# An edge-attention layer on one core: gathers two to three pairs ahead in two buffers, attributes loaded from ScalarE's queue

## The chip, the cores and the metric

The kernel runs on one core of one Trainium2 chip. The metric is the time of one execution in device microseconds (us); a kernel's time is the median of its runs. The engines are named as in the profile: PE (TensorE, matmuls), PEld (its weight loads), DVE (VectorE), ACT (ScalarE), POOL (GpSimd) and SP (SyncE, which here only issues DMAs). "SPq" and "ACTq" are the DMA queues of SP and ACT.

## The reference

A graph layer over 12500 nodes of 128 channels and 400000 edges, which come sorted by their target (dst), while their sources (src) are in no order:

```python
h = jnp.maximum(_layernorm(x), 0)
msg_src = h @ w_src + b_src
msg_dst = h @ w_dst
message = msg_src[edge_src] + msg_dst[edge_dst]
rad_w = mlp3(edge_attr_32)            # 32 -> 64 -> 64 -> 128, silu between
message = message * edge_weight1 * rad_w
message = message @ w_sep + b_sep     # 128 -> 256
alpha, value = split(message.reshape(E, 8, 32))    # 16 + 16 in each of 8 heads
score = einsum('ehk,ahk->eh', smooth_leaky_relu(alpha), alpha_dot)
att = segment_softmax(score, edge_dst)
out = segment_sum(value * att, edge_dst).reshape(N, 128)
return x + out @ w_proj + b_proj
```

(Names shortened; mlp3 and split stand for what the reference writes out.) For each edge a row of msg_src has to be fetched by an index (the gather), a row of msg_dst is found nearby, because the targets are sorted, and 32 attributes go through a small network.

## The kernel before

Three phases follow each other. Up to about 110 us the two node tables are made (t_src, t_dst) and the limits of the windows of targets are found. Then `windows()` goes over the edges; this phase ends near 5700 us and is the one that the change touches. Last, the sums of windows that share targets are put together and the output product is made.

`windows()` works on 400 pairs k of 1000 edges. A pair has two sections f of 500 edges, each with a window of at most 64 rows of targets, and a section is four tiles of 125 edges. The order of the work is written out by hand in `step(k)`, which runs for k = -5 to 399 and then for a few steps more: every call in it appends its instructions to the engines' queues, in that order. A step handles several pairs at different stages:

- Loads for later pairs, issued by SP at the step's start: the edge weights `load_w(k + 3)` (L718), the two windows of target rows `load_md(k + 3)` (tile md, L720 to L724; SP reads each window's start from a table first), for every second k the target indices `load_d` (tile d_b), and the attributes `load_e(k + 6)` (tile e_t, L705 to L707; 1000 runs of 128 bytes).
- `gather(k, f)` (L739 to L747): four indirect DMAs issued by POOL (L744), each of which fetches 125 rows of t_src into the tile gs0 or gs1. It is called for pair k + 4, section 1, after the transposes of pair k, section 1, and for pair k + 5, section 0, after those of pair k + 1, section 0.
- The network of the attributes: `e_T` for k + 3 (PE transposes of e_t into m1, ACT copy), `mlp1` for k + 2 (L763, ACT silu into h, L766), `mlp2` for k + 1 (L778, L781) and `mlp3` for k (L795), whose result DVE multiplies by the edge weights (rad, L799).
- `split_md` (L726 to L737): the target rows of k + 1 are split in three bf16 parts, two by ACT (L730, L735) and two subtractions by DVE (L733, L737).
- `sources` (L808): PE transposes the gathered rows into the PSUM tiles pm0, pm1; `message` adds the target rows by one-hot products (L816), and DVE makes mT from pm and rad (L821).
- `alphas(k, f)`: the product pa (L825), ACT's silu into sl (L827), DVE's al (L829); it is called for section 0 in the middle of the step and for section 1 near its end. `scores` (every second step) makes the scores of two pairs and SP writes them out (L841).
- The softmax runs per group of 8 pairs (MP = 8). 12 steps later (pair c = k - 12) `values` (V, L908; pvx, L910), `one_hot` and `sums` (L919; ACT copy ob, L923) are made, and SP stores the sums, `store_win` (L927) and `store` (L931, tile agg).

Each tile's name has a fixed number of buffers (`bufs`): a new tile of that name reuses the oldest buffer, and its first writer waits until the former tile's last reader is done. Before the change e_t has 4, md has 4, gs0 and gs1 have 4 each. A DMA also waits for the one that was issued eight earlier of its kind (SP's and ACT's together, POOL's apart), since eight completion semaphores are used in turn.

The order in `step` around the change is:

```python
if has(k + 3):
    load_w(k + 3)
    load_md(k + 3)
if k % 2 and has(k + 3):
    load_d((k + 3) // 2)
if has(k + 6) and k >= -4:
    load_e(k + 6)
```

Of the kernel before, what the change touches and what calls it, by code (L numbers as in the profile page):

```python
# [21 lines left out]
F32 = mybir.dt.float32  # L22
# [8 lines left out]
P = 128  # L31
C = 128
# [14 lines left out]
TS = 4  # L47
# [9 lines left out]
def gnn_kernel(ctx: ExitStack, tc: tile.TileContext, a: dict, out: bass.AP):  # L57
    nc = tc.nc
# [69 lines left out]
    def zero(i):  # L128

        av = agg[0:N, :].rearrange("(p t) c -> p (t c)", p=RP)  # L130
        nc.sync.dma_start(out=av[:, i * zc * ROW:(i + 1) * zc * ROW], in_=z)
        if i == 0:
            nc.sync.dma_start(out=agg[N:N + W, :], in_=z[:W, 0:ROW])
# [527 lines left out]
    def windows():  # L661
        src_t = src.rearrange("(t p) -> t p", p=T)
        dst_t = dst.rearrange("(t p) -> t p", p=T)
        ea_t = ea.rearrange("(k j p) c -> k p j c", j=8, p=T)
        dst_p = dst.rearrange("(k f e) -> f k e", f=2, e=SEC)
        ew_p = ew.rearrange("(k e) o -> o k e", e=PR)
        with tc.tile_pool(name="wk2", bufs=2) as sp, tc.tile_pool(name="ps", bufs=1, space=PSUM) as pp, \
                tc.manual_schedule(), ExitStack() as held:
            lp = held.enter_context(tc.tile_pool(name="ld", bufs=2))
            prep, e_g, d_g, w_g, md, gath = {}, {}, {}, {}, {}, {}  # L670
# [4 lines left out]
            def prep_load(u):  # L675
                t0 = u * P
                ri = lp.tile([P, 2, T], I32, name="ri")
                rb = lp.tile([P, 1], I32, name="rb")
                nc.sync.dma_start(out=ri[:, 0, :], in_=src_t[t0:t0 + P, :])
                nc.sync.dma_start(out=ri[:, 1, :], in_=dst_t[t0:t0 + P, :])  # L680
                at = dst_t[t0:t0 + P, 0:1]
                (step, _), *_ = at.ap
                at = bass.AP(at.tensor, at.offset, [[step * TS, P // TS], [0, TS], [1, 1]])
                with nc.allow_non_contiguous_dma(reason="a word per tile"):
                    nc.sync.dma_start(out=rb, in_=at)
                prep[u] = (ri, rb)
# [17 lines left out]

            def load_e(k):  # L705
                e_g[k] = lp.tile([T, 8, RAD], F32, name="e_t", bufs=4)
                nc.sync.dma_start(out=e_g[k], in_=ea_t[k])  # L707

            def load_d(g):
                d_g[g] = lp.tile([P, 2, SEC], I32, name="d_b")  # L710
                for f in range(2):
                    nc.sync.dma_start(
                        out=d_g[g][f * W:(f + 1) * W],
                        in_=dst_p[f:f + 1, 2 * g:2 * g + 2, :].to_broadcast([W, 2, SEC]))

            def load_w(k):
                w_g[k] = lp.tile([P, PR], F32, name="w_b", bufs=4)
                nc.sync.dma_start(out=w_g[k], in_=ew_p[:, k, :].to_broadcast([P, PR]))  # L718

            def load_md(k):  # L720
                md[k] = lp.tile([P, C], F32, name="md", bufs=4)
                at = [nc.sync.value_load(base[0:1, f, k:k + 1]) for f in range(2)]
                for f in range(2):
                    nc.sync.dma_start(out=md[k][f * W:(f + 1) * W, :], in_=t_dst[ds(at[f], W), :])  # L724
# [12 lines left out]
                    nc.vector.tensor_sub(m3[k][:, 2, :], mr.pop(k), m3[k][:, 1, :])  # L737

            def gather(k, f):  # L739
                gs = lp.tile([P, TS, C], F32, name=f"gs{f}", bufs=4)  # L740
                idx, _ = prep[k // 16]
                for j in range(TS):
                    t = k % 16 * 8 + f * TS + j
                    nc.gpsimd.indirect_dma_start(  # L744
                        out=gs[:, j, :], out_offset=None, in_=t_src[:, :],
                        in_offset=bass.IndirectOffsetOnAxis(ap=idx[:, t:t + 1], axis=0))
                gath[k, f] = gs  # L747
# [75 lines left out]
            def alphas(k, f):  # L823
                pa = pp.tile([C, SEC], F32, name="pa")
                nc.tensor.matmul(pa, w_a, mTs[k][:, f * SEC:(f + 1) * SEC], start=True, stop=True)  # L825
                sl = sp.tile([C, SEC], F32, name="sl")
                nc.scalar.activation(sl, pa, AF.Silu, bias=b_a, scale=1.0)  # L827
                al = sp.tile([C, SEC], F32, name="al", bufs=6)
                nc.vector.scalar_tensor_tensor(al, pa, 0.25, sl, op0=ALU.mult, op1=ALU.add)  # L829
                als[2 * k + f] = al  # L830
# [18 lines left out]
            def load_sm(m):  # L849
                sms[m] = sp.tile([P, SEC + 1], BF16, name="sm")  # L850
                at = same[0:1, m * MQ * SEC:m * MQ * SEC + 1]
                at = bass.AP(at.tensor, at.offset, [[SEC, MQ], [0, H], [1, SEC + 1]])
                nc.sync.dma_start(out=sms[m], in_=at)
# [72 lines left out]
            def store_win(c):  # L926
                nc.sync.dma_start(out=win[c * P:(c + 1) * P, :], in_=accs[c])  # L927

            def store(c, f):
                at = nc.sync.value_load(base[0:1, f, c:c + 1])  # L930
                nc.sync.dma_start(out=agg[ds(at, W - 1), :], in_=accs[c][f * W:(f + 1) * W - 1, :])  # L931


            def load_x(i):
                xs[i] = lp.tile([P, 4, C], F32, name="xs")
                for n, t0, t1 in blocks(*quads[i]):
                    o = quads[i][0]
                    nc.sync.dma_start(out=xs[i][:n, t0 - o:t1 - o, :],
                                      in_=x_v[:, t0:t1, :] if n == P else x[NF * P:N, :].unsqueeze(1))
# [8 lines left out]
            def has(k):  # L948
                return 0 <= k < NP
# [3 lines left out]
            for k in range(2):  # L953
                load_e(k)
            def step(k):
                c = k - LAG
                if has(c - 1):
                    store_win(c - 1)
                    store(c - 1, 0)

                if k % 16 == 4 and has(k + 12):
                    prep_load((k + 12) // 16)
                if has(k + 3):
                    load_w(k + 3)
                    load_md(k + 3)
                if k % 2 and has(k + 3):
                    load_d((k + 3) // 2)
                if has(k + 6) and k >= -4:
                    load_e(k + 6)
                if has(k + 4) and (k + 4) % MP == 0:  # L970
                    load_sm((k + 4) // MP)
                if has(c - 1):
                    store(c - 1, 1)
                if 0 <= 2 * k < NZ:
                    for i in range(2 * k, min(2 * k + 2, NZ)):
                        zero(i)
                if k % 16 == 8 and has(k + 8):
                    prep_make((k + 8) // 16)
                i, q = divmod(k - 40, MP)
                if 0 <= i < Q and q == 0:  # L980
                    load_x(i)
                if 0 <= i < Q and q == 7:
                    add_x(i)
                if has(k + 1):
                    split_md(k + 1, 0)
                if has(c):
                    weights(c)
                rad = mlp3(k) if has(k) else None
                if has(k):
                    sources(k, 1)  # L990
                if has(k + 4):
                    gather(k + 4, 1)
                if has(k):
                    message(k, rad)
                if has(c):
                    values(c, 0)
                if has(k + 1):
                    split_md(k + 1, 1)
                if has(k):
                    alphas(k, 0)  # L1000
                if has(k + 1):
                    split_md(k + 1, 2)
                if has(k + 2):
                    mlp1(k + 2)
                if has(c):
                    values(c, 1)
                    one_hot(c)

                if has(k + 1):
                    sources(k + 1, 0)  # L1010
                if has(k + 5):
                    gather(k + 5, 0)
                if has(k):
                    alphas(k, 1)
                if has(k + 1):
                    mlp2(k + 1)
                    one_hot_T(k + 1)
                    split_md(k + 1, 3)
                if has(c):
                    sums(c)  # L1020
                m, r = divmod(k, MP)
                if has(k - MP):
                    if r == 1:
                        softmax_up(m - 1)
                    elif r == 2:
                        softmax_down(m - 1)
                        softmax_exp(m - 1)
                    elif r == 3:
                        softmax_T(m - 1)
                if has(k + 3):  # L1030
                    e_T(k + 3)
                if has(k) and k % 2 == 1:
                    scores(k)

            for k in range(-5, NP):
                step(k)
# [184 lines left out]
    with tc.tile_pool(name="fin", bufs=3) as fp, tc.tile_pool(name="fin1", bufs=1) as f1, \  # L1221
# [7 lines left out]
        gs, qs, qTs, has = {}, {}, {}, {}  # L1229
# [104 lines left out]
```

## Time and profile before

| what | value |
|---|---|
| median of 3 runs | 5886.15 us (5853.44 to 5887.58) |
| profiled execution, its own time | 5892.37 us |
| its span | 5890.6 us |
| mean granted clock of TensorE | 0.892 |
| DMA | 794.76 MB, mean 135 GB/s |
| DMA packets | 901338, of which 530271 under 512 bytes |

The share of the 16 DMA engines that the queues take is 36.4% for SP's (q1) and 17.9% for POOL's (q0), by the page's table of queues. In the page's table of slices (40 slices of 147 us) PE is at 0.7 to 0.8 through the windows phase, POOL at 0.5, DMA at 0.5.

In a line of the timeline the columns are the start, the duration, the engine, the source line, the operation, the tile written and the tiles read, how many instructions are put together (x), and in brackets the idle time of the engine just before with what ended it. "issue" means that the engine waited for nothing that the profile shows, "remote" that what ended the wait isn't known. In the view of one tile the three numbers are the least, the median and the longest duration in ns, then the first and last start in us.

### The profile page before, as it was taken

How to read it: one execution, taken by the hardware profiler on the slowest of the kernel's cores; microseconds unless marked ns; L12 is line 12 of the kernel's file. 1: busy time of each engine (PE TensorE's matmuls, PEld its weight loads, DVE VectorE, ACT ScalarE, POOL GpSimd, SP SyncE). 2: the span in 40 equal slices, each digit the busy share in tenths (PEclk: the TensorE clock that was granted, in tenths of full speed). 3: DMA queues.
4: the chain of work that ended last, by engine and by line, in shares of the span. 5: the costliest groups of instructions: out<-in, count | busy, mean ns of one | idle time of the engine just before them, and what ended most of it. 6: DMA issues, size and time to landing. Idle time of an engine off the chain costs nothing.

```text
span 5890.6 us, 88077 instructions
## 1 busy us (share of the span) xinstructions
PE 4616.9 (78%) x29692; PEld 2541.0 (43%) x29692; DVE 3100.6 (53%) x6005; ACT 1909.7 (32%) x4595; POOL 3119.2 (53%) x3223
## 2 busy tenths in 40 slices
PE   5688788787877788777877887787887887787874
PEld 3244444444444444444444444444444444444444
DVE  5345555555555555555555554555555555455566
ACT  4233333333333333333333333333333333333331
POOL 1655555555555555555555555555555555555520
PEclk8788988898989999899898998999998989888897
DMA  5565555555555555555565555555555555555533
GB/s 194 156 142 133 136 129 135 139 138 128 143 129 139 144 131 135 132 138 132 137 139 132 140 132 129 128 132 131 137 130 135 127 132 136 127 132 127 132 89 143
DMA packets 901338, 794.76 MB, mean 135 GB/s; under 512 B 530271, under 2 KB 776975, under 8 KB 900747
## 3 DMA queue, kind: packets, MB, share of 16 engines
q1 hardware_dynamic: 796664, 572.15, 36.4%
q0 software_dynamic: 102816, 210.37, 17.9%
q10 hardware_dynamic: 1394, 6.53, 0.3%
q8 instruction: 234, 3.83, 0.3%
q14 instruction: 230, 1.88, 0.1%
HBM read 648.39 MB, written 140.67 MB: 134 GB/s over the span
## 4 chain that ended last, share of the span: by engine, by line
PE 70%; another core or an unknown queue 9%; DVE 8%; issue 7%; ACT 4%; DMA 1%; SPq 1%; POOL 0%; ACTq 0%; POOLq 0%; DVEq 0%
PE V L908 14%; PE pa L825 13%; PE pm L808 8%; PE p L795 8%; PE misc L919 7%; PE pm L816 5%; PE misc L836 4%; PE p L763 4%; PE p L778 4%; PE m L754 3%; DVE mT L821 2%; DVE rad L799 2%; DVE pvx L910 1%; ACT sl L827 1%
## 5 line engine op out<-in xcount | busy, mean ns | idle before, releaser
L744 POOL DMA_INDIRECT gs<-t_src,idx x3200 | 3104.8, 970 | 2537.2 <-PE pm L808 1152.5
L827 ACT ACTIVATE sl<-pa,c_b_a 128x500 f32<-128x500 f32 x800 | 541.9, 677 | 2419.9 <-PE pa L825 1302.9
L825 PE MATMUL pa<-mT,c_w_a 128*128 128x500 f32 x1600 | 933.4, 668 | 451.4 <-DVE mT L821 276.0
L908 PE MATMUL V<-c_w_v,mT 128*125 128x128 f32 x6208 | 987.6, 307 | 198.3 <-DVE pvx L910 171.7
L799 DVE SCALAR_TENSOR_TENSOR rad<-p,c_fc_b,w_b 128x500 f32<-128x500 f32 x800 | 553.2, 733 | 1096.5 <-PE p L795 623.9
L908 PEld LDWEIGHTS V<-c_w_v,mT 128*125 128x125 f32 x6208 | 829.3, 207 | 518.7 <-issue 274.7
L829 DVE SCALAR_TENSOR_TENSOR al<-pa,sl 128x500 f32<-128x500 f32 x800 | 542.3, 678 | 654.3 <-ACT sl L827 396.0
L910 DVE TENSOR_TENSOR pvx<-V,Pem 125x512 f32<-125x512 f32 x776 | 533.2, 687 | 588.7 <-remote 180.6
L821 DVE SCALAR_TENSOR_TENSOR mT<-pm,c_b_src,rad 128x500 f32<-128x500 f32 x800 | 555.1, 733 | 207.4 <-remote 112.2
L919 PE MATMUL misc<-pvx,oh 125*64 125x136 f32 x6400 | 475.7, 292 | 123.2 <-DVE oh L898 75.1
L808 PE MATMUL pm<-ident,gs 125*128 125x125 f32 x3200 | 561.2, 303 | 1.6 <-DMA gs<-t_src,idx 1.6
L808 PEld LDWEIGHTS pm<-ident,gs 125*128 125x128 f32 x3200 | 404.3, 156 | 343.9 <-issue 341.6
L795 PE MATMUL p<-h,w3b 64*128 64x500 f32 x1600 | 495.8, 699 | 34.5 <-ACT h L781 27.1
L919 PEld LDWEIGHTS misc<-pvx,oh 125*64 125x64 f32 x6400 | 372.2, 141 | 290.1 <-issue 183.1
L825 PEld LDWEIGHTS pa<-mT,c_w_a 128*128 128x128 f32 x1600 | 267.7, 210 | 511.0 <-DVE mT L821 310.9
L836 PE MATMUL misc<-al,w_s 128*32 128x500 f32 x1600 | 243.5, 679 | 236.9 <-ACT ob L923 122.9
L816 PE MATMUL pm<-ohT,m 64*128 64x500 bf16 x2400 | 340.6, 392 | 0.0
L763 PE MATMUL p<-eT,w1b 64*128 64x250 f32 x1600 | 309.4, 467 | 1.0 <-ACT eT L756 1.0
L923 ACT COPY ob<-misc 128x136 f32<-128x136 f32 x400 | 109.0, 273 | 619.4 <-PE m L754 308.2
L781 ACT ACTIVATE h<-p,b 128x500 f32<-128x500 f32 x400 | 269.8, 674 | 97.5 <-remote 77.4
L778 PE MATMUL p<-h,w2b 64*64 64x250 f32 x3200 | 278.7, 421 | 9.2 <-ACT h L766 7.7
L766 ACT ACTIVATE h<-p,b 128x500 f32<-128x500 f32 x400 | 272.9, 682 | 27.3 <-remote 14.9
(145 smaller groups left out, 3259.2 us busy)
## 6 DMA issues: line engine op xcount, KB each, us to landing
w_b<-in_edge_weight SPq DMA_DIRECT2D x400, 500.0 KB
d_b<-in_dst SPq DMA_DIRECT2D x400, 250.0 KB
gs<-t_src,idx POOLq DMA_INDIRECT x3200
e_t<-in_edge_attr SPq DMA_DIRECT2D x400, 125.0 KB
sc_d<-Sp SPq DMA_DIRECT2D x200, 250.0 KB
win<-ob SPq DMA_DIRECT2D x400, 68.0 KB
agg<-ob SPq DMA_DIRECT2D x800, 33.5 KB
md<-t_dst SPq DMA_DIRECT2D x800, 32.0 KB
```

Source lines behind the costliest of these rows:

```text
L744: nc.gpsimd.indirect_dma_start(out=gs[:, j, :], out_offset=None, in_=t_src[:, :], in_offset=bass.IndirectOffsetOnAxis(ap=idx[:, t:t + 1], ...
L763: nc.tensor.matmul(p1[:, q, 0:2 * T], w1b[s, :], eTs[k][s, :], start=True, stop=True)
L795: nc.tensor.matmul(p3[:, f, 0:SEC], w3b[s, :], h2s[k][s, :], start=True, stop=True)
L799: nc.vector.scalar_tensor_tensor(rad[:, s], p3[:, f, 0:SEC], b3, w_g[k][:, s], op0=ALU.add, op1=ALU.mult)
L808: nc.tensor.matmul(pms[k, f][:, t * T:(t + 1) * T], gs[:T, t, :], ident[:T, :T], start=(t == 0), stop=False, is_transpose=True, skip_group ...
L816: nc.tensor.matmul(pm[f], m3[k][s, j, :], ohT[k][s, :], start=False, stop=(j == 2), skip_group_check=True)
L821: nc.vector.scalar_tensor_tensor(mTs[k][:, s], pm[f], b_n, rad[:, s], op0=ALU.add, op1=ALU.mult)
L825: nc.tensor.matmul(pa, w_a, mTs[k][:, f * SEC:(f + 1) * SEC], start=True, stop=True)
L827: nc.scalar.activation(sl, pa, AF.Silu, bias=b_a, scale=1.0)
L908: nc.tensor.matmul(V[:, t, :], mTs[c][:, o:o + T], w_v, start=True, stop=True)
L910: nc.vector.tensor_mul(pvx[c][:, f, :, 0:C].rearrange("p t (h k) -> p t h k", h=H), V.rearrange("p t (h k) -> p t h k", h=H), Pem[c // MP] ...
L919: nc.tensor.matmul(acc[f * W:(f + 1) * W, :], ohs[c][:, f * TS + t, :], pvx[c][:, f, t, :], start=(t == 0), stop=(t == TS - 1), skip_group ...
```

## The change

Five edits. The attributes' load is issued by ACT in place of SP, and its call stands after `alphas(k, 0)` in place of the step's start. The target rows are loaded four pairs ahead in place of three, with five buffers in place of four. The gathers are issued two pairs (section 1) and three pairs (section 0) ahead in place of four and five, and gs0 and gs1 have two buffers each in place of four.

```diff
             def load_e(k):
                 e_g[k] = lp.tile([T, 8, RAD], F32, name="e_t", bufs=4)
-                nc.sync.dma_start(out=e_g[k], in_=ea_t[k])
+                nc.scalar.dma_start(out=e_g[k], in_=ea_t[k])
...
             def load_md(k):
-                md[k] = lp.tile([P, C], F32, name="md", bufs=4)
+                md[k] = lp.tile([P, C], F32, name="md", bufs=5)
...
             def gather(k, f):
-                gs = lp.tile([P, TS, C], F32, name=f"gs{f}", bufs=4)
+                gs = lp.tile([P, TS, C], F32, name=f"gs{f}", bufs=2)
...
                 if has(k + 3):
                     load_w(k + 3)
-                    load_md(k + 3)
+                if has(k + 4):
+                    load_md(k + 4)
                 if k % 2 and has(k + 3):
                     load_d((k + 3) // 2)
-                if has(k + 6) and k >= -4:
-                    load_e(k + 6)
...
                 if has(k):
                     sources(k, 1)
-                if has(k + 4):
-                    gather(k + 4, 1)
+                if has(k + 2):
+                    gather(k + 2, 1)
                 if has(k):
                     message(k, rad)
...
                 if has(k):
                     alphas(k, 0)
+                if has(k + 6) and k >= -4:
+                    load_e(k + 6)
                 if has(k + 1):
                     split_md(k + 1, 2)
...
                 if has(k + 1):
                     sources(k + 1, 0)
-                if has(k + 5):
-                    gather(k + 5, 0)
+                if has(k + 3):
+                    gather(k + 3, 0)
```

## The prediction

> **What bounds the kernel now.** I read the page first (busy times, chain that ended last), then the waits of SP and POOL, the tiles that the change touches, and last two stretches of the timeline, one of an ordinary pair and one of the start.
>
> ```profile
> span 5890.6 us, 88077 instructions
> PE 4616.9 (78%) x29692; PEld 2541.0 (43%) x29692; DVE 3100.6 (53%) x6005; ACT 1909.7 (32%) x4595; POOL 3119.2 (53%) x3223
> PE 70%; another core or an unknown queue 9%; DVE 8%; issue 7%; ACT 4%; DMA 1%; SPq 1%; POOL 0%; ACTq 0%; POOLq 0%; DVEq 0%
> L744 POOL DMA_INDIRECT gs<-t_src,idx x3200 | 3104.8, 970 | 2537.2 <-PE pm L808 1152.5
> ```
>
> PE's chain of matmuls is the bound: it is busy 78% of the span and carries 70% of the chain. DMA ends 1% of it, SP's queue 1%, and POOL, which issues the gathers, nothing. From one radial product (rad, L799) to the next pair's, a pair takes 13.9 us on average over the 400 pairs. POOL is idle mostly because it waits for PE to release a slot (PE pm, L808 is the transpose that reads a gathered tile), not the reverse.
>
> ```profile
> SPq L841 <- ACT m L730: 875.6, 151, 9.9
> POOL gs L744 <- PE pm L808: 1152.5, 314, 9.4
> ```
>
> These come from the waits of SP and of POOL (us, times, longest). SP's largest wait, 875.6 us, is for the scores at the end of a pair (L841): SP runs ahead and then sits. Time saved on SP is worth nothing while this holds.
>
> ```profile
> L744 POOL DMA_INDIRECT gs<-t_src,idx x3200: 939/947/1642, 114.6 to 5643.2; - x189
> L707 SPq DMA_DIRECT2D e_t<-in_edge_attr x400: 3/464/1830, 111.4 to 5619.7; - x134
>   DMA gs<-t_src,idx: 11.7, 9
>   DMA e_t<-in_edge_attr: 2.4, 2
> ```
>
> From the views of tiles gs and e_t: a gather's issue takes 947 ns of POOL and an attributes' load 464 ns of SP (median); the last two lines are the idle time that their arrivals end anywhere, 11.7 us and 2.4 us. No data is late now.
>
> **The change part by part.** The sum is made against the profiled execution: 5892.37 us, span 5890.6, 1.8 us around it; it stands 6.2 us above the median of the runs, 5886.15.
>
> *Gathers nearer to their use, half the buffers.* The same 3200 gathers are issued in the same places among POOL's and PE's instructions. With four buffers a section's gather for pair k+4 reuses the slot of pair k, with two that for k+2 does too: each still follows directly the transposes that free its slot. So POOL's wait for PE stays, and only the lead shrinks. In the trace the last of a section's four gathers is issued 41.4 us before PE reads the tile at the least, 49.8 at the median; two pairs less (2 x 13.9 = 28) leaves some 14 to 22 us, an estimate. From issue to landing a gather takes 4.7 us at the median and 9.9 at the worst of all 3200. So it still lands before its use: cost 0. If the least lead met the worst landing with a burst of four (5 us) between, 14 against 15, a rare microsecond would show: some 0 to 20 us over the span. I take 0.
>
> *The start.* Here the number of free slots matters. Timeline:
>
> ```profile
> 128.89 1.39 DVE L799 SCALAR_TENSOR_TENSOR rad<-p,c_fc_b,w_b 128x500 f32<-128x500 f32 x2 [1.81 <-PE pm L808]
> 151.20 0.74 DVE L821 SCALAR_TENSOR_TENSOR mT<-pm,c_b_src,rad 128x500 f32<-128x500 f32 x1 [20.92 <-remote]
> 160.38 0.68 ACT L827 ACTIVATE sl<-pa,c_b_a 128x500 f32<-128x500 f32 x1 [28.64 <-remote]
> 163.57 0.95 POOL L744 DMA_INDIRECT gs<-t_src,idx  x1 [0.30 <-issue]
> 172.15 0.95 POOL L744 DMA_INDIRECT gs<-t_src,idx  x1 [7.64 <-remote]
> 175.35 1.38 DVE L799 SCALAR_TENSOR_TENSOR rad<-p,c_fc_b,w_b 128x500 f32<-128x500 f32 x2 [1.41 <-issue]
> ```
>
> POOL issues 40 gathers back to back, 1.25 us apart, from 114.6 to 163.6 us: all that four slots allow. While that lasts, everything else crawls: mT waits 20.92 us and sl 28.64 us for something that the profile doesn't name ("remote"), though the matmuls they need are done, and the first pair takes 175.35 - 128.89 = 46.5 us where an ordinary one takes 13.9. It ends when the burst does. The chain of waits of this stretch says the same:
>
> ```profile
> 131.75 28.61 another core or an unknown queue
> ```
>
> With two slots the gathers of pairs 0 and 1 and what the first two transposes release are free, 24 in place of 40: 16 x 1.25 = 20 us less of the burst. The pair can't give more than 46.5 - 13.9 = 32.6 us, and gives 0 if the crawl has another cause (the first loads of all kinds also run then). I take 20: the waits end with the burst.
>
> *The end.* Before, the last gather is issued at 5643.2 us, so that pairs 396 to 398 run beside none: 9.3, 10.3 and 8.6 us by the starts of rad. With the shorter lead, gathers go on for two pairs more. In the places that 396 and 397 have in the groups of eight the means are 11.1 and 16.0 us, so up to 1.8 + 5.7 = 7.5 us is lost, at least 0. I take 5, as most of what is quick in these pairs goes with the gathers.
>
> *Attributes' load on ScalarE.* It leaves SP's group at a pair's start and stands in ScalarE's order behind the first sl of the pair, ahead of the cast of m (L735), h (L766) and the second sl; no instruction of PE, DVE or POOL moves. An ordinary pair:
>
> ```profile
> 3011.02 0.51 SPq L707 DMA_DIRECT2D e_t<-in_edge_attr  x1
> 3011.04 0.68 ACT L827 ACTIVATE sl<-pa,c_b_a 128x500 f32<-128x500 f32 x1 [4.72 <-PE pa L825]
> 3011.61 0.29 ACT L735 CAST m<-mr 128x128 bf16<-128x128 f32 x1
> 3012.18 0.68 ACT L766 ACTIVATE h<-p,b 128x500 f32<-128x500 f32 x1 [0.28 <-PE p L763]
> 3012.35 2.98 SPq L931 DMA_DIRECT2D agg<-ob  x1
> 3015.07 0.68 ACT L827 ACTIVATE sl<-pa,c_b_a 128x500 f32<-128x500 f32 x1 [2.21 <-PE pa L825]
> ```
>
> An issue on ScalarE is bounded by those it makes already, x_fin's (L1227) at the end, 0.33 to 0.70 us, by e_t's own on SP, 0.464, and by the DMA that follows it there, agg, here 2.98 us and 7.2 at the most, against 0.35 for agg elsewhere. I take 0.464: on ScalarE nothing is issued behind it. Ahead of the second sl ScalarE is idle 2.2 us here (2.0 at the median, 0.33 at the least), so the cast and h come half a microsecond later and the second sl on time: 400 x 0.464 = 186 us are hidden, and are the price if that cover goes. The load's waits are its tile's reader, two pairs back, and the DMA eight issues earlier, which lies in the step before: landed by then. It stays six pairs ahead, and one slip of a few us doesn't reach PE. SP gains 400 x 0.464 and some 2 us a pair behind it, and waits longer for the scores: 0.
>
> A page of the Trainium skill speaks against this part: "Perfetto Trace Analysis", in the section on the HWDGE instruction, has the descriptor generator shared by the issuing sequencers and locked by one at a time, the wait for the lock being the issuer's. By it ScalarE could have to wait for the agg issue in progress: (2.98 + 0.46 - 2.2) x 400 = 500 us more if it met one every time, an estimate; by the rows above, 0. The rows that I read show no issue of ScalarE beside one of SP.
>
> *Rows of targets four pairs ahead.* Same loads and registers, 14 us earlier on SP. They land at most 8.0 us after issue and are asked for 40 us ahead; their arrival ends 4.2 us of idle time in all. Gain 0 to 4, I take 0.
>
> Sum: 5892.4 - 20 + 5 = 5877.4 by the profiled execution, and 5886.15 - 15 = **5871 us** by the median.
>
> **The rivals.**
>
> *ScalarE becomes late (slower).* The load stands ahead of h and of the second sl, which DVE's al, the release of pa and, through it, PE's next products wait for. For: ScalarE already sits 534 us ahead of sl in waits that end in "issue", where its sequencer and not data is late, and in the burst at the start SP's steps are 0.70 us apart, so a load of several steps on a crawling ScalarE costs more than 0.46. Against: 2 us of idle time ahead of the second sl. From 0.2 us shown a pair it eats the gain and passes 1% (0.2 x 400 = 80); shown in half or in full, the time is 5871 + 93 = 5964 to 5871 + 186 = 6057.
>
> *SP was clogged (faster).* agg's issue behind e_t takes 2 to 7 us, and 9% of the chain, 530 us, is put down to an unknown queue. If a part of this is SP's stores and loads held up behind 1000 small pieces of e_t, freeing SP gives SP's 1% of the chain, 59 us, to a quarter of the unknown, 133: 5871 - 59 = 5812 to 5738. Against: SP's 875.6 us of waiting, and almost no idle time that a DMA ends. The Trainium skill's first page, "Trainium Kernel Development and Optimization", under Key Constraints, is against it too: all queues share the 16 DMA engines, and several issuers save only issue time.
>
> *The start gives nothing, or the end takes it back.* 5886 to 5894, no change that can be told. For: the crawl has no named cause.
>
> *Gathers come late (slower).* Decides from a landing of 14 us; at the 9.9 seen it doesn't occur. With 1 us in each pair it would be 5871 + 400 = 6271.
>
> **How the numbers follow.** About 1% (59 us) is what a measurement of this kernel can tell from no change. Forecast (its own range 5845 to 5890, from 0 to 32.6 us at the start, 0 to 7.5 at the end, and some slips): 0.47. Start gives nothing: 0.08. SP was clogged: 0.22. ScalarE late: 0.19. Gathers late: 0.04. So faster 0.22, same 0.55, slower 0.23. The range takes in the first two (0.55), two thirds of the third, down to 5812 - 2/3 x (5812 - 5738) = 5763, and half of the fourth, spread from 5951 to 6057, up to 6004: 0.55 + 0.15 + 0.09 = 0.79.
>
> **What would show it.** In the profile after: POOL's first burst ends near 144 us and the first pair takes about 26 us; the idle time that gs ends stays under 30 us; the load on ScalarE is near 0.46 us with sl's idle time ahead of it shorter by as much; the sum of sl's waits for "issue" stays near 534. I am wrong if the load on ScalarE lasts over 2 us, if PE's idle time ahead of L808 grows, or if the pairs in mid-span differ from 13.9 us by more than 0.1.

## The result, and the profile after

| | before | after |
|---|---|---|
| median | 5884.87 us (4 runs, 5853.44 to 5887.58) | 5811.88 us (4 runs, 5804.92 to 5816.74) |
| ratio | | 0.9881, 95% interval 0.985 to 0.9912 |
| profiled execution, its span | 5892.37, 5890.6 us | 5814.39, 5812.6 us |

The experiments ran on four chips, of two kinds: on that of the first set the kernel before takes 5866 us, on the three others 4583 to 4628, with the same instructions. Which chip made the comparison above isn't on record; by its 5885 us it is of the first kind. A ratio is always to the kernel before in the same comparison; I call the chips "slow" and "quick" below.

The page after (span; busy times; queues; chain; the group of the gathers):

```profile
span 5812.6 us, 87691 instructions
PE 4590.1 (79%) x29692; PEld 2537.5 (44%) x29692; DVE 3082.3 (53%) x6005; ACT 1903.7 (33%) x4595; POOL 3127.7 (54%) x3223
...
q1 hardware_dynamic: 394664, 520.94, 30.1%
...
q10 hardware_dynamic: 403394, 57.74, 6.6%
...
PE 70%; DVE 9%; issue 9%; another core or an unknown queue 6%; ACT 4%; DMA 2%; SPq 0%; ACTq 0%; DVEq 0%
...
L744 POOL DMA_INDIRECT gs<-t_src,idx x3200 | 3113.2, 973 | 2470.6 <-PE pm L808 988.1
```

The work is the same; half of the packets have gone from SP's queue (q1) to ScalarE's (q10). In the chain the unknown part went from 9% to 6% (about 530 to 350 us), "issue" from 7% to 9%. By the starts of rad, where the 78 us of span went:

| stretch | before | after | difference |
|---|---|---|---|
| up to the first rad | 128.9 | 135.8 | +6.9 |
| first pair (0 to 1) | 46.5 | 20.0 | -26.5 |
| pairs 1 to 8 | 88.7 | 103.7 | +15.0 |
| pairs 8 to 396 | 5392.5 | 5309.8 | -82.7 |
| pairs 396 to 399 | 28.2 | 35.7 | +7.5 |
| the rest | 205.9 | 207.6 | +1.7 |

The middle of the span brought the gain; the start, on balance, brought 4.5 us. The middle's pairs went from 13.90 to 13.68 us, and most of it is in one of the eight places that a pair can have in its group: k mod 8 = 5 went from 16.0 to 12.9 us and k mod 8 = 1 from 13.8 to 13.0, while k mod 8 = 4 lost part of that again (11.1 to 12.7).

The waits of SP and of POOL, and the tiles gs and e_t:

```profile
SPq L841 <- ACT m L730: 1379.3, 147, 14.8
```

```profile
POOL gs L744 <- PE pm L808: 988.1, 302, 15.3
```

```profile
L744 POOL DMA_INDIRECT gs<-t_src,idx x3200: 942/947/1643, 117.1 to 5585.1; - x189
...
  DMA gs<-t_src,idx: 13.7, 10
```

```profile
L707 ACTq DMA_DIRECT2D e_t<-in_edge_attr x400: 266/267/2654, 107.9 to 5527.6; - x134
```

SP waits 504 us longer for the scores: it is earlier than before (what that is worth, an experiment below tells). The gathers end 13.7 us of idle time (11.7 before), so the shorter lead is long enough. The load costs ScalarE 267 ns at the median, where it cost SP 464. The start in the timeline:

```profile
135.83 1.38 DVE L799 SCALAR_TENSOR_TENSOR rad<-p,c_fc_b,w_b 128x500 f32<-128x500 f32 x2 [5.11 <-issue]
...
141.08 0.94 POOL L744 DMA_INDIRECT gs<-t_src,idx  x1 [0.30 <-issue]
...
145.38 0.94 POOL L744 DMA_INDIRECT gs<-t_src,idx  x1 [3.36 <-remote]
...
147.47 1.39 DVE L821 SCALAR_TENSOR_TENSOR mT<-pm,c_b_src,rad 128x500 f32<-128x500 f32 x2 [10.26 <-remote]
...
155.79 1.38 DVE L799 SCALAR_TENSOR_TENSOR rad<-p,c_fc_b,w_b 128x500 f32<-128x500 f32 x2 [0.48 <-PE p L795]
```

```profile
238.04 0.27 ACTq L707 DMA_DIRECT2D e_t<-in_edge_attr  x1
238.35 0.30 ACT L735 CAST m<-mr 128x128 bf16<-128x128 f32 x1 [15.93 <-DMA e_t<-in_edge_attr]
```

The burst of gathers stops at 142 us and the first pair ends at 155.8. The second fence is from the step of pair 6, whose rad is 24.8 us ahead of the next: ScalarE stands still for 15.93 us ahead of the cast, because the load ahead of it waits for an earlier load of attributes on the same semaphore, issued at 209.3 us and landed at 238.0 beside the stores that zero the sums; h, sl and with them PE wait behind it. An ordinary pair, where the load is free:

```profile
2959.43 0.27 ACTq L707 DMA_DIRECT2D e_t<-in_edge_attr  x1
...
2960.00 0.29 ACT L735 CAST m<-mr 128x128 bf16<-128x128 f32 x1
2960.57 0.68 ACT L766 ACTIVATE h<-p,b 128x500 f32<-128x500 f32 x1 [0.28 <-issue]
...
2963.40 0.68 ACT L827 ACTIVATE sl<-pa,c_b_a 128x500 f32<-128x500 f32 x1 [2.15 <-PE pa L825]
```

The second sl is still preceded by 2.15 us of idle time.

### The profile page after: what moved, and what is told of

The parts are those of the page before. It is cut to its first block, busy times and chain, and to the rows that moved or that the text cites. A ratio compares the mean times of both kernels' runs of the same rounds, so it can differ in the third digit from the quotient of the medians.

```text
span 5812.6 us, 87691 instructions
## 1 busy us (share of the span) xinstructions
PE 4590.1 (79%) x29692; PEld 2537.5 (44%) x29692; DVE 3082.3 (53%) x6005; ACT 1903.7 (33%) x4595; POOL 3127.7 (54%) x3223
## 4 chain that ended last, share of the span: by engine, by line
PE 70%; DVE 9%; issue 9%; another core or an unknown queue 6%; ACT 4%; DMA 2%; SPq 0%; ACTq 0%; DVEq 0%
PE pa L825 13%; PE V L908 13%; PE misc L919 8%; PE p L795 7%; PE pm L808 7%; PE pm L816 6%; PE p L763 4%; PE misc L836 4%; PE p L778 4%; PE m L754 3%; DVE mT L821 3%; DVE rad L799 2%; DVE pvx L910 1%; PE misc L880 1%
## 5 line engine op out<-in xcount | busy, mean ns | idle before, releaser
L825 PE MATMUL pa<-mT,c_w_a 128*128 128x500 f32 x1600 | 899.6, 646 | 389.4 <-DVE mT L821 305.1
L795 PE MATMUL p<-h,w3b 64*128 64x500 f32 x1600 | 487.6, 689 | 13.9 <-ACT h L781 7.7
## 6 DMA issues: line engine op xcount, KB each, us to landing
agg<-ob SPq DMA_DIRECT2D x800, 33.5 KB
```

What stands on the lines that cost most here:

```text
L795: nc.tensor.matmul(p3[:, f, 0:SEC], w3b[s, :], h2s[k][s, :], start=True, stop=True)
```

## The experiments

My theory after the result: the load of the attributes, 1000 pieces of 128 bytes, clogged SP's queue, and SP was late although it waited much in sum (the queue theory). Rivals: the nearer gathers did it, as POOL's runs of seven and more gathers back to back (at most 1.6 us from one's start to the next) fell from 101 to 23; or the load's place in the pair; or its traffic on the DMA engines.

**One part at a time, on the slow chip** (12 runs each, 35 of the kernel before, 5866.24 us).

Gathers alone:

```diff
-gs = lp.tile([P, TS, C], F32, name=f"gs{f}", bufs=4)
+gs = lp.tile([P, TS, C], F32, name=f"gs{f}", bufs=2)
-gather(k + 4, 1) ... gather(k + 5, 0)
+gather(k + 2, 1) ... gather(k + 3, 0)
```

> Only the gathers' part of the change (two buffers, two and three pairs ahead). If the queue of the attributes' load is the cause of the gain in mid-span, only the start and the end remain: pairs in mid-span stay at 13.9 us, the first pair falls from 46.5 to about 20, the end loses 7: ratio 0.996 to 0.999. If the gathers' lead is the cause (POOL's bursts no longer merge: 100 runs of seven or more gathers back to back before, 23 after), a pair in mid-span takes 13.7 us and the ratio is 0.986 to 0.990.

Measured 5860.22 us, ratio 0.999 (0.996 to 1.002). The rad of pair 8 came 15.2 us earlier (264.1 to 248.9), the first pair took 28.4 us, and pairs 396 to 399 took 32.0 us in place of 28.2. Start and end moved as expected, each by less, and give 11 us in all. In the middle there is no gain that can be told: its profile has 13.80 us a pair, and the interval takes in 1.

The load on ScalarE, at its new place:

```diff
-nc.sync.dma_start(out=e_g[k], in_=ea_t[k])
+nc.scalar.dma_start(out=e_g[k], in_=ea_t[k])
 # and load_e(k + 6) called after alphas(k, 0)
```

> Only the attributes' load on ScalarE, at its new place. Queue theory: mid-span pairs at 13.7 us, the pairs with k mod 8 = 5 at about 12.9 in place of 16.0, start as before; ratio 0.985 to 0.989. Gathers' theory: mid-span 13.9, ratio 0.997 to 1.003. ScalarE's cost, if it showed, would make it slower than 1.002.

Measured 5824.5 us, ratio 0.9941 (0.9912 to 0.997). In its profile pairs 8 to 392 take 13.69 us each, k mod 8 = 5 takes 13.5; the rad of pair 8 is 16.1 us late (280.2 for 264.1). A smaller gain than the theory said (0.985 to 0.989), with the sign it said; the start, later and not as before, eats part of it.

Only the place, SP still issuing:

```diff
 # load_e(k + 6) called after alphas(k, 0); nc.sync as before
```

> Only the place of the load is changed, SP still issues it, now behind the second store of the sums and not ahead of it. Queue theory: no change, 0.997 to 1.003, the class k mod 8 = 5 near 16.0. If it is the load's place among SP's stores that matters (nothing behind it in the same pair), it gives the whole gain, 0.985 to 0.990.

Measured 5878.06 us, ratio 1.0017 (0.9989 to 1.0044): the place alone gives nothing. But its profile, of the slowest of the 12 runs, shows something else. At the later place SP's next DMA mostly comes over 2 us behind the load, and is no longer held up:

```profile
3006.69 0.30 SPq L707 DMA_DIRECT2D e_t<-in_edge_attr  x1
3009.83 0.34 SPq L927 DMA_DIRECT2D win<-ob  x1
```

```profile
SPq L841 <- ACT m L730: 1443.5, 162, 14.0
```

The rows right behind the loads take 273 us in sum, 974 in the kernel before, and SP waits 1443.5 us for the scores in place of 875.6, as much as after the whole change (1379.3). So SP is earlier, and on the slow chip nothing comes of it: SP's held-up time isn't what the change gains there.

ScalarE, but at the step's start:

```diff
-nc.sync.dma_start(out=e_g[k], in_=ea_t[k])
+nc.scalar.dma_start(out=e_g[k], in_=ea_t[k])
 # load_e(k + 6) called where it was
```

> The load on ScalarE, but called at the step's start, so ahead of the first sl and the casts. Queue theory: the same gain as at the new place, 0.985 to 0.990. If its time within the pair decides, no gain or a loss: 0.997 to 1.01, with sl of section 0 (idle 3.5 us ahead of it) hiding the issue either way.

Measured 5856.22 us, ratio 0.9989 (0.9954 to 1.0023). Its profiled execution, one of its quickest (5833), has the pairs of the kernel above (13.69) and the same late start; over all runs it is no gain that can be told. So on the slow chip the place counts too, and the queue theory isn't enough there. Single runs of one kernel spread over 50 to 90 us here.

**The whole change and its parts, on a quick chip** (5 runs each, kernel before 4583.25 us).

> The whole change once more, beside its parts. If the parts add up, gathers 0.999 and the load on ScalarE 0.994 give 0.993 (0.990 to 0.996). If they strengthen each other, 0.988 as in the first comparison.

Measured 4465.83 us, ratio 0.9746 (0.973 to 0.9761): over twice the gain that it has on the slow chip, and outside both ranges, which came from there.

The change without its target rows part:

```diff
-md[k] = lp.tile([P, C], F32, name="md", bufs=5)
+md[k] = lp.tile([P, C], F32, name="md", bufs=4)
...
-if has(k + 4):
-    load_md(k + 4)
+    load_md(k + 3)      # under if has(k + 3), behind load_w(k + 3)
```

> The change without its target rows part: these three pairs ahead and in four buffers, as before. If that part does nothing, the same ratio as the whole change within 0.003. If the earlier load of the rows matters (its registers and two loads lie elsewhere in SP's order at a group's start), the ratio is 0.004 or more above that of the whole change.

Measured 4469.27 us, ratio 0.9754 (0.9738 to 0.9769): that part does nothing that can be told.

No loads of attributes after the fourth pair:

```diff
-e_g[k] = lp.tile([T, 8, RAD], F32, name="e_t", bufs=4)
+if k >= 4:
+    e_g[k] = e_old[k % 4]
+    return
+e_g[k] = e_old[k] = lp.tile([T, 8, RAD], F32, name=f"e_t{k}", bufs=1)
```

> The kernel before with the attributes loaded for the first four pairs alone; later pairs use these four tiles again, so 396 of the 400 loads are left out. If the gain comes from SP's queue being free of this load, this gives at least what the load on ScalarE gives: ratio 0.985 to 0.994, mid-span pairs 13.7 us or less. If the load's traffic on the DMA engines is what slows the pairs, clearly more: 0.97 to 0.985. If neither, 0.998 to 1.002.

Measured 4432.3 us, ratio 0.9672 (0.9656 to 0.9688), below both ranges, which were made from the slow chip; so it is the profile that decides between the theories. The kernel, which leaves out 396 loads, is 33.5 us quicker than the whole change, and 31 of them are in the start (rad of pair 8 at 214.1 us for 245.0). Pairs 8 to 392 take 10.27 us in both: in the middle the whole change has all that can be had from this load, and the load's traffic costs nothing there.

The first six loads on SP again:

```diff
-nc.scalar.dma_start(out=e_g[k], in_=ea_t[k])
+(nc.sync if k < 6 else nc.scalar).dma_start(out=e_g[k], in_=ea_t[k])
```

> The whole change, but the loads of the first six pairs are issued by SP as before; the others by ScalarE. The first rad was 7 us later in the profile after and 14 us later with the load on ScalarE alone, where ScalarE's issues took 2.5 to 3.1 us each and stood ahead of its copies. If these cost the start that much, this is 7 to 14 us faster than the whole change, ratio 0.001 to 0.0025 lower; if the burst of gathers hides it, no difference.

Measured 4471.51 us, ratio 0.9755 (0.974 to 0.9771): not faster. The first rad does come earlier (128.6 for 132.2), but pair 6 takes 29.3 us all the same (27.5 in the whole change on this chip). It is a later load, issued by ScalarE, that waits:

```profile
232.29 0.30 ACT L735 CAST m<-mr 128x128 bf16<-128x128 f32 x1 [20.43 <-DMA e_t<-in_edge_attr]
```

**The kernel before on a quick chip**, for its profile.

> The kernel before itself, for a profile on another chip: the second comparison ran 22% faster on its chip (before 4583 us in place of 5866), with pairs of 10.3 us in the changed kernel and none of the waits that end in 'remote'. If this lies in the chip, a profile of the kernel before shows there what the load on SP costs without those stalls: by the queue theory pairs of some 10.6 us with SP late (its waits for the scores near nothing), by the traffic theory PE waiting at the transposes for gathers or attributes. On a chip like the first one, pairs of 13.8 us again.

Measured 4583.33 us. Pairs 8 to 392 take 10.61 us; in the whole change on the other quick chip they take 10.27, and 384 x 0.34 = 131 us is the gain there, of which the start takes 16 back. The page's span and chain, ScalarE's longest wait for data, and two of SP's issues:

```profile
span 4581.5 us, 88077 instructions
...
PE 60%; DMA 13%; DVE 8%; SPq 8%; ACT 6%; issue 4%; POOL 1%; ACTq 0%; POOLq 0%; DVEq 0%
```

```profile
ACT m L730 <- DMA md<-t_dst: 808.6, 294, 10.4
```

```profile
2525.26 0.51 SPq L707 DMA_DIRECT2D e_t<-in_edge_attr  x1
2526.59 3.12 SPq L931 DMA_DIRECT2D agg<-ob  x1
```

This is what the queue theory says: the target rows, loaded three pairs ahead, come too late 294 times, since SP, which issues them, is behind. From SP's issue to ScalarE's read the rows have 3.7 us at the median in the middle of the span, against 23 on the slow chip. What holds SP up should be the issue behind e_t: agg's takes 3.12 us here, 2.70 at the median, 887 us over the 334 pairs in which it follows e_t, against 0.34 elsewhere. There is no large wait for the scores on SP any more (its longest in sum is 30.5 us). The whole change on a quick chip, the same two lines of its page:

```profile
span 4466.3 us, 87691 instructions
...
PE 79%; DVE 7%; DMA 5%; ACT 4%; issue 3%; SPq 1%; POOL 0%; ACTq 0%; POOLq 0%; DVEq 0%
```

SP's part of the chain fell from 8% to 1%, DMA's from 13% to 5%, and PE carries 79%.

**Fewer, larger pieces.** Each partition now holds four neighbouring edges of each section. First on top of the change:

```diff
-ea_t = ea.rearrange("(k j p) c -> k p j c", j=8, p=T)
+ea_t = ea.rearrange("(k f p j) c -> k p f (j c)", f=2, j=4, p=T)
...
-nc.scalar.dma_start(out=e_g[k], in_=ea_t[k])
+nc.scalar.dma_start(out=e_g[k].rearrange("p (f j) c -> p f (j c)", f=2), in_=ea_t[k])
...
-nc.scalar.activation(h2s[k].rearrange("x (q h p) -> x h q p", q=2, h=2),
+nc.scalar.activation(h2s[k].rearrange("x (p q h) -> x h q p", q=2, h=2),
```

> The change, and the attributes loaded in 250 runs of 512 bytes a pair in place of 1000 of 128: a partition holds four neighbouring edges of each section, and the second silu writes its columns in the edges' order again (stride of four). If the number of small pieces is the cost of this load, on the DMA engines or in the queue, this nears the kernel without the loads: 0.007 below the whole change. If only the place in SP's queue was the cost, as the whole change within 0.002; if ScalarE's strided write is slow, worse by 0.01 or more.

Measured 4452.27 us, ratio 0.971 (0.9692 to 0.9728), on the chip of the profile above (4585.74): 0.0036 below the whole change on another chip, between the two cases. The pairs in the middle don't change (10.27 us), as ScalarE's load holds up nothing there; the start does: the rad of pair 8 at 232.1 us in place of 245.0 in the whole change.

The same pieces in the kernel before, with SP issuing at the old place:

> The kernel before, its attributes still loaded by SP at the old place, but in 250 runs of 512 bytes a pair in place of 1000 of 128 (the second silu writes with a stride of four). On a chip where the kernel before takes 4583 us: if it is the small pieces that hold up SP, ScalarE's waits for md (808.6 us in its profile there) go nearly all, pairs of 10.3 us, ratio 0.970 to 0.977. If one more issue a pair on SP is what makes it late, whatever its pieces, 0.985 to 1.0. On a chip where it takes 5866 us: 0.990 to 0.998 by the first, 0.998 to 1.003 by the second.

Measured 4443.12 us on a third quick chip, where the kernel before takes 4628.2: ratio 0.9603 (0.959 to 0.9616), lower than expected, as the kernel before is slower on this chip. SP's issues in its timeline, ScalarE's wait for md, and the second silu in the view of tile h:

```profile
2507.85 0.46 SPq L707 DMA_DIRECT2D e_t<-in_edge_attr  x1
2509.07 0.36 SPq L931 DMA_DIRECT2D agg<-ob  x1
```

```profile
ACT m L730 <- DMA md<-t_dst: 21.3, 8, 7.5
```

```profile
L781 ACT ACTIVATE h<-p,b x400: 1141/1187/1482, 130.4 to 4231.4; 128x500 f32<-128x500 f32 x134
```

agg's issue behind e_t is 0.35 us at the median, 117 us in sum: 770 us of SP's time come back with no change of queue, buffers or lead, the rows of targets have 13.9 us at the median again, and 808.6 us of ScalarE's waits for them have become 21.3. So on quick chips it was the pieces, and one more issue a pair on SP costs nothing that shows. The silu's strided write takes 1187 ns for 672, and the pairs are at 10.28 us all the same. It is the quickest time of all kernels that do the whole work, ahead of both kernels compared; on the slow chip it wasn't run.

The load on ScalarE alone, beside it on the same chip:

> Once more only the attributes' load on ScalarE at its new place, the gathers four and five pairs ahead and the target rows three, as before. On a chip where the kernel before takes 4583 us: by the queue theory all of the gain of the whole change (0.9746 there), 0.973 to 0.977, ScalarE's waits for md under 50 us. If the nearer gathers have a part in it, 0.980 or more. On a chip where it takes 5866 us: 0.994 again, 0.991 to 0.997.

Measured 4478.21 us, ratio 0.9675 (0.9662 to 0.9689). Lower than expected, as the kernel before is slower on this chip; the time is within 13 us of the whole change's on another. What its cast of md (L730), and the subtraction behind it, wait for, in the view of tile md:

```profile
its engine sat idle before it (us, times) until:
  ACT m L730: 7.9, 1
```

There is no line of a DMA left: the cast's 808.6 us of waits for md are gone, with the gathers and the rows of targets as they were (these have 14.4 us at the median). On quick chips the change is the move of this one load. The larger pieces on SP are 35 us ahead of it on the same chip, and that is the start: pairs 8 to 392 take 10.28 and 10.30 us, but the rad of pair 8 comes at 216.3 and 256.0 us.

## Why the prediction was right or wrong

The time, 5811.88 us, lies in the range and moved the way that was forecast, but by 73 us where I had 15, and outside the forecast's own 5845 to 5890. The range took it in through its share of the rival "SP was clogged" (5738 to 5812), whose edge it meets by 0.1 us. That is in part luck: the rival's cause is shown on the quick chips, and on the slow one SP's freed time brought nothing. Of the signs of being wrong one came, pairs of 13.68 us in mid-span in place of 13.9; and sl's waits for "issue", which were to stay near 534 us, are 653.9.

- *The start.* 20 us for the shorter burst: the first pair fell by 26.5, and with the gathers alone by 18 (46.5 to 28.4) and 15.2 up to pair 8. Right in place and size on a slow chip. The cause given isn't all: on a quick chip the kernel before issues its first 56 gathers back to back, until 184.6 us, and the first pair, in the midst of them, takes 9.1 us, so a burst by itself makes nothing crawl; what the slow chip adds to it isn't known.
- *The end.* 5 us, measured 7.5; with the gathers' lead as before it stays at 28.2 us exactly.
- *Gathers' lead.* Cost 0: 13.7 us of idle time for 11.7, with a lead of 16.9 us at the least in mid-span, where the estimate was 14 to 22. Right.
- *The load on ScalarE.* 0.464 us, hidden: measured 0.267 and hidden in the ordinary pair, so the rival "ScalarE becomes late" fell in the middle of the span. In the start the sentence "landed by then" failed: once the DMA eight issues earlier, a load of attributes in flight for 28.7 us, wasn't landed, and ScalarE stood for 15.9 us with PE behind it; with the 6.9 us before the first rad it took back 22 of the 26.5 us.
- *The page on the HWDGE instruction*, "Perfetto Trace Analysis" of the Trainium skill, has an issue wait for the shared generator. In the middle of the span no such wait shows: 267 ns at the median, and 244 of the issues there overlap one of SP in time and take at most 286 ns. The 500 us that it could have cost didn't come.
- *Rows of targets.* 0: the whole change with and without it differs by 0.0008 with intervals twice that, on a quick chip. Right. From issue to ScalarE's read, which the prediction put at 40 us, it is 23 us at the median before the change and 37 after.
- *SP's gain: 0, and so no gain in mid-span.* This is the term that failed. The load on ScalarE alone, on the slow chip, gave 42 us (5866.24 to 5824.5) and mid-span pairs of 13.69 us for 13.90. The reason given for the 0, that SP waits 875.6 us and so its time is worth nothing, held on the slow chip as far as the runs show: the load at its later place let SP wait 1443.5 us, and the time didn't fall. The gain there has another cause, which stays open. On the quick chips the reason itself fails. The pairs that other stalls stretch to 13.9 us on the slow chip take 10.6 there, SP has no such wait left, and its 887 us behind e_t are the bound. The row was in the prediction's lines, agg's issue of 2.98 us right behind e_t against 0.33 elsewhere (2.1 at the median, 810 us in sum), and was put at 0.
- *Key Constraints* on the first page of the Trainium skill, that several issuers save only issue time, agrees with the runs: agg's issues take 282 us in sum with the load on ScalarE, 1046 with it on SP, and on quick chips that was worth having.

What stays open: how, on the slow chip, the load's leaving SP shortens pairs that stand in waits for something "remote". A pair of k mod 8 = 5 before looks so:

```profile
3447.21 0.74 DVE L821 SCALAR_TENSOR_TENSOR mT<-pm,c_b_src,rad 128x500 f32<-128x500 f32 x1 [2.93 <-remote]
...
3451.61 0.68 ACT L827 ACTIVATE sl<-pa,c_b_a 128x500 f32<-128x500 f32 x1 [8.50 <-remote]
```

md isn't late there (4.2 us in the whole span). Long runs of gathers don't explain these stalls: only 167 of the 797 us of them (each over 1 us, on ScalarE and DVE, from 180 to 5600 us) fall beside runs of seven or more, which fill 19% of that time. On quick chips 128 gathers run back to back without one, and on the slow chip the gathers' part alone and the place alone cut the long runs to half or less (41 and 50 for 101) without a gain in the middle. The parts (0.999 and 0.9941, product 0.993) and the whole (0.9881) differ by no more than their intervals allow; whether they add up on the slow chip isn't settled either.

## What to carry to other kernels

A DMA's own issue row doesn't show what it costs its queue: look at the row of the next DMA behind it, for each tile, and at how soon that one comes. A queue's waiting in sum is slack only while the loop keeps its pace: ask what it would be with the loop at its best pace. And before moving a load of many small pieces to another engine, make the pieces larger: here that gave as much in the middle and more at the start, for 0.5 us more of ScalarE a pair.

## What the runs showed of the hardware

- The same program takes 5866 us on one chip and 4583 to 4628 on three others, with the granted clock near 0.90 and 0.97. On the slow kind even SP's register moves are held up. The view of tile md, before on a slow chip and on a quick one:

```profile
L724 SPq MOVE md<-t_dst x800: 2/29/857, 119.2 to 5660.5; - x160
```

```profile
L724 SPq MOVE md<-t_dst x800: 29/29/42, 120.2 to 4359.7; - x160
```

  The median is the same 29 ns, the longest 857 and 42. A gather's issue (970 and 977 ns in the mean) and sl's silu (677 on both) take as long on both, and PE's matmuls 4617 and 4196 us in sum; most of the difference is in waits between engines. The cause wasn't found.
- agg's DMA, issued by SP right behind a load of 1000 pieces of 128 bytes (1.3 us after its start), took 2.1 to 2.7 us at the median and up to 7.2; behind 250 pieces of 512 bytes 0.35 and at most 0.39. With the load at its later place, where the next DMA of SP mostly came 2 us or more behind it, that one took 0.35 us too. The load's own issue took ScalarE 0.267 us, and SP 0.464 at the step's start and 0.287 at the later place.
- "DMA: Bandwidth & Descriptors" of the Trainium skill, in its table of specifications, gives 512 bytes as the least piece at full rate. The runs agree as far as they go: at 512 bytes the hold-up is gone and q1's packets fall by 300000; with ScalarE issuing, the share of the DMA engines that its queue takes falls from 8.9% to 5.0%.
